# A fused RWKV, Mamba and feed-forward block on one core: in its first phase the reciprocal by Ln and Exp with a Newton step, the sigmoid by itself, the layer norm scaled by ScalarE, and the table lookups split seven to four

## The chip, the cores and the metric

The kernel runs on one core of one Trainium2 chip. A core has five engines with instruction queues of their own, each working in order: TensorE (PE, with its weight loads shown as PEld), VectorE (DVE), ScalarE (ACT), GpSimd (POOL) and SyncE (SP), which here issues the DMAs. An instruction that waits holds up all that is queued behind it on its engine. The metric is the device time of one execution in microseconds. Before the change the median of 3 runs is 3853.84 us (3852.79 to 3855.59).

## The reference

The input `x` has 4096 tokens (2 sequences of 2048) of 512 channels. Four residual parts follow each other, each behind a layer norm: an RWKV attention, a feed-forward, a Mamba, and the same feed-forward again. What the change touches is in the first part and in the weights of the second:

```python
def step(carry, kv):                       # RWKV, along the tokens
    p, q, o = carry
    kt, vt = kv
    no = jnp.maximum(o, u + kt)
    A = jnp.exp(o - no)
    Bc = jnp.exp(u + kt - no)
    y = (A * p + Bc * vt) / (A * q + Bc)
    no2 = jnp.maximum(w + o, kt)
    A2 = jnp.exp(w + o - no2)
    B2 = jnp.exp(kt - no2)
    return ((A2 * p + B2 * vt, A2 * q + B2, no2), y)
...
rvk = jnp.einsum('btc,dc->btd', x, W_rvk)
r, v, k = jnp.split(rvk, 3, axis=-1)
y = jax.nn.sigmoid(r) * wkv(time_decay, time_first, k, v)
return jnp.einsum('btc,dc->btd', y, W_out)
...
def _ghost_linear(x, idx, lut):            # feed-forward: weights from a table of 16 numbers
    w = lut[idx]
    return jnp.einsum('bsh,oh->bso', x, w)
...
h = jax.nn.silu(gate) * up
```

All tensors are float32. The denominator `A * q + Bc` is positive.

## The kernel before

The program has two phases. The second (Mamba and both feed-forwards, 16 chunks of 256 tokens, an order written out by hand with due times) is not touched. The first phase does the RWKV part in 8 chunks of 512 tokens (`TA`), and a scheduler orders its instructions on each engine, from the order of the code and its own estimates of durations.

A chunk begins with `layernorm_T`: DVE takes the statistics of four tiles of 128 tokens (L89, L90), POOL forms the reciprocal root `rs` (L91, L92), DVE scales the rows to `xn` (L95), PE transposes them (L98), ACT copies them to `xnT` (L99). Then a loop over `c` takes four groups of 128 channels; one pass of it is called a block here, and blocks are counted through from 0 to 31. In a block:

- PE projects k, r and v into PSUM (L293, 24 matmul passes);
- ACT takes `er` = exp(-r) (L303);
- DVE scans the running maximum `o` (L316) and forms `e`, the difference that all exponents come from (L320);
- ACT makes four Relu and Exp pairs from `e`: `b2`, `a2`, `bb`, `aaS` (L323 to L330), and copies `aaS` to `aa` in PSUM (L331);
- DVE multiplies with v (L333 `bv`, L334 `vb`) and scans p and q (L335, L336); ACT carries the last column on (L337, L312);
- POOL forms the numerator in `vb` (L339, L340);
- DVE forms the denominator in `aa` (L341, L342), multiplies it by 1 + `er` (L343), so that one reciprocal (L344) serves the division and the sigmoid together, and writes `yT` (L345).

At the end of a chunk PE multiplies `yT` with `wout` (L351), DVE adds to `x` (L353), and SP stores the chunk.

Beside that, the phase prepares the feed-forward's weights for the second phase: 11 pieces (`NF`) of 128 x 1536 indices are looked up in the table of 16 numbers and stored to DRAM as `wff`. There are two ways. `lookup` does it by bits on DVE: four masks from the index bits (L158), one product of masks (L161), and a nest of and/xor with polynomial coefficients (L167 to L184), 23 operations on 128 x 1536 integers. `lookup_pe` does it by products: DVE compares the indices with each of the values 0 to 15 (L211, one step each), and PE adds up nine matmuls for each step (L214) with diagonal matrices that hold three bfloat16 pieces of the table's numbers. Both are generators; `put`, called at the end of each block, takes so many steps of each as `lots` says. In the last four blocks `feed_forward` puts the first 256 tokens through the feed-forward (L248, L254, L238).

PSUM holds five buffers `mm` (k, r, v, `a2`, `aa` of a block in turn; also the transposes and the output products) and three `lk`. The tile pool `wk` holds eleven buffers for the other intermediates; `opq` (o, p, q) has two.

Of the kernel before, what the change touches and what calls it, by code (L numbers as in the profile page):

```python
# [8 lines left out]
F32 = mybir.dt.float32  # L9
I32 = mybir.dt.int32  # L10
AF = mybir.ActivationFunctionType
ALU = mybir.AluOpType
# [3 lines left out]
P = 128  # L16
# [5 lines left out]
NF = (FF + P - 1) // P  # L22
# [38 lines left out]
def block_kernel(ctx: ExitStack, tc: tile.TileContext, a: dict, out: bass.AP):  # L61
    nc = tc.nc
    V, S, G, PE = nc.vector, nc.scalar, nc.gpsimd, nc.tensor
# [18 lines left out]
    def layernorm_T(xt, n, xnT, small, new_xn, trp):  # L82


        st = small.tile([P, n, 6], F32, tag="st", name="st")
        mv = small.tile([P, n, 2], F32, tag="mv", name="mv")
        rs = small.tile([P, n, 1], F32, tag="rs", name="rs")
        for j in range(n):
            V.bn_stats(st[:, j, :], xt(j))  # L89
            V.bn_aggr(mv[:, j, :], st[:, j, :])  # L90
        G.tensor_scalar(rs, mv[:, :, 1:2], EPS, None, ALU.add)  # L91
        G.tensor_tensor(rs[:, :, 0], rs[:, :, 0], mhalf[:, :n], ALU.pow)  # L92
        for j in range(n):
            xn = new_xn()
            V.tensor_scalar(xn, xt(j), mv[:, j, 0:1], rs[:, j, :], ALU.subtract, ALU.mult)  # L95
            tr = trp.tile([P, KC, P], F32, tag="mm", name="tr")
            for k in range(KC):
                PE.transpose(tr[:, k, :], xn[:, k * P : (k + 1) * P], ident)  # L98
            S.copy(xnT[:, :, j * P : (j + 1) * P], tr)  # L99


    with ExitStack() as pa:
# [3 lines left out]
        small = pa.enter_context(tc.tile_pool(name="a_small", bufs=2))  # L106
# [20 lines left out]
        def load_x(i):  # L127
            xt = xp.tile([P, TA // P, C], F32, tag="x", name="x")
            nc.sync.dma_start(
                xt, a["x"][i * TA : (i + 1) * TA, :].rearrange("(j p) c -> p j c", p=P)  # L130
            )
            return xt
# [89 lines left out]
        def feed_forward():  # L222
# [4 lines left out]
            nc.sync.dma_start(xt, x1)  # L227
            xnT = lp.tile([P, KC, TB], F32, tag="fT", name="fT")
            layernorm_T(lambda j: xt[:, j, :], nj, xnT, small,
                        lambda: xnp.tile([P, C], F32, tag="xn", name="xn"), mmp)  # L230
            yield
# [32 lines left out]
        def each(how, part):  # L264
            for i in part:
                yield from how(i)

        lots = [(each(lookup, range(0, NF, 2)), 30, 0, 27), (each(lookup_pe, range(1, NF, 2)), 80, 0, 28),
                (feed_forward(), NF + 1, 28, 31)]

        def put(block):
            for steps, n, lo, hi in lots:
                if lo <= block < hi:
                    for _ in range(n * (block - lo) // (hi - lo), n * (block + 1 - lo) // (hi - lo)):
                        next(steps, None)
                if block == hi - 1:
                    for _ in steps:
                        pass
# [3 lines left out]
        for ci in range(nchunk):  # L282
            xt = first if ci == 0 else load_x(ci)
            xnT = xp.tile([P, KC, TA], F32, tag="xnT", name="xnT")
            layernorm_T(lambda j: xt[:, j, :], TA // P, xnT, small,
                        lambda: xnp.tile([P, C], F32, tag="xn", name="xn"), mmp)
            yT = xp.tile([P, KC, TA], F32, tag="yT", name="yT", bufs=1)
            for c in range(KC):
                def proj(which):
                    ps = mmp.tile([P, TA], F32, tag="mm", name="ps")  # L290
                    lo = which * C + c * P
                    for k in range(KC):
                        PE.matmul(ps, lhsT=wrvk[:, k, lo : lo + P], rhs=xnT[:, k, :],  # L293
                                  start=(k == 0), stop=(k == KC - 1))
                    return ps

                def t(name):
                    return wk.tile([P, TA], F32, tag="wk", name=name)

                k_ps, r_ps, v_ps = proj(2), proj(0), proj(1)  # L300
                w1 = wcol[:, c : c + 1]
                er = t("er")
                S.activation(er, r_ps, AF.Exp, scale=-1.0)  # L303

                st3 = wk.tile([P, 3, TA + 1], F32, tag="opq", name="opq", bufs=2)
                o, pp, qq = (st3[:, d, :] for d in range(3))
                if ci % (SEQ // TA) == 0:
                    V.memset(o[:, 0:1], -1e38)
                    V.memset(pp[:, 0:1], 0.0)
                    V.memset(qq[:, 0:1], 0.0)  # L310
                else:
                    S.copy(st3[:, :, 0], car[:, :, c])  # L312
                if c == 0:
                    nxt = carp.tile([P, 3, KC], F32, tag="car", name="car")
                old, new = slice(0, TA), slice(1, TA + 1)
                V.tensor_tensor_scan(o[:, new], w1.to_broadcast([P, TA]), k_ps, o[:, 0:1],  # L316
                                     ALU.add, ALU.max)

                e = t("e")
                V.scalar_tensor_tensor(e, o[:, old], w1, k_ps, ALU.add, ALU.subtract)  # L320
                a2, aa = (mmp.tile([P, TA], F32, tag="mm", name=n) for n in ("a2", "aa"))
                b2, bb, aaS = t("b2"), t("bb"), t("aaS")
                S.activation(b2, e, AF.Relu)  # L323
                S.activation(b2, b2, AF.Exp, scale=-1.0)
                S.activation(a2, e, AF.Relu, scale=-1.0)
                S.activation(a2, a2, AF.Exp, scale=-1.0)
                S.activation(bb, e, AF.Relu, bias=nwu[:, c : c + 1])
                S.activation(bb, bb, AF.Exp, scale=-1.0)
                S.activation(aaS, e, AF.Relu, bias=wu[:, c : c + 1], scale=-1.0)
                S.activation(aaS, aaS, AF.Exp, scale=-1.0)  # L330
                S.copy(aa, aaS)  # L331
                bv, vb = t("bv"), t("vb")
                V.tensor_tensor(bv, b2, v_ps, ALU.mult)  # L333
                V.tensor_tensor(vb, bb, v_ps, ALU.mult)  # L334
                V.tensor_tensor_scan(pp[:, new], a2, bv, pp[:, 0:1], ALU.mult, ALU.add)  # L335
                V.tensor_tensor_scan(qq[:, new], a2, b2, qq[:, 0:1], ALU.mult, ALU.add)  # L336
                S.copy(nxt[:, :, c], st3[:, :, TA])  # L337

                G.tensor_tensor(aaS, aaS, pp[:, old], ALU.mult)  # L339
                G.tensor_tensor(vb, aaS, vb, ALU.add)  # L340
                V.tensor_tensor(aa, aa, qq[:, old], ALU.mult)  # L341
                V.tensor_tensor(aa, aa, bb, ALU.add)  # L342
                V.scalar_tensor_tensor(aa, er, 1.0, aa, ALU.add, ALU.mult)  # L343
                V.reciprocal(aa, aa)  # L344
                V.tensor_tensor(yT[:, c, :], vb, aa, ALU.mult)  # L345
                put(KC * ci + c)
            car = nxt
            for j in range(TA // P):
                po = mmp.tile([P, C], F32, tag="mm", name="po")
                for k in range(KC):  # L350
                    PE.matmul(po, lhsT=yT[:, k, j * P : (j + 1) * P], rhs=wout[:, k, :],  # L351
                              start=(k == 0), stop=(k == KC - 1))
                V.tensor_tensor(xt[:, j, :], xt[:, j, :], po, ALU.add)  # L353
            nc.sync.dma_start(x1d[ci].rearrange("(j p) c -> p j c", p=P), xt)


    with ExitStack() as pb:
# [13 lines left out]
        small = pb.enter_context(tc.tile_pool(name="b_small", bufs=2))  # L371
# [437 lines left out]
        for w in range(-1, nchunk + 1):  # L809
            t = SLOTS * w  # L810
# [85 lines left out]
```

## Time and profile before

| | |
|---|---|
| median of 3 runs | 3853.84 us (3852.79 to 3855.59) |
| profiled execution | 3854.41 us |
| its span | 3852.6 us, 44708 instructions |
| busy in the span: PE, DVE, POOL, ACT | 93%, 84%, 71%, 67% |
| first phase, 0 to 805 us: PE, DVE, ACT, POOL busy | 706.7, 674.6, 256.2, 106.6 us |

A line of the page's chain of waits gives the lines on the way that ended last; a group line gives a source line, engine, operation, output and input tile with their shapes, the count, then busy time and mean nanoseconds of one, then the idle time of the engine just ahead of it and what ended that. Busy time counts overlapping instructions once, so that a group's busy time can be below its count times its mean. The 40 digits of an engine are its busy share in tenths in 40 equal slices of the span.

### The profile page before, as it was taken

To read this page: it belongs to the slowest core of one execution; us is meant where nothing else is said; L and a number is where in the kernel's file an instruction comes from. 1 tells how busy PE (TensorE), PEld (TensorE's weight loads), DVE (VectorE), ACT (ScalarE), POOL (GpSimd) and SP (SyncE) were. 2 spreads that over 40 slices of the span, in tenths; PEclk is the share of its full clock that TensorE was granted. 3 is DMA by queue.
4 is the path that set the end of the run, shared out by engine and by line. 5 is a ranking of instruction groups with operands and counts; after the bars stand their busy time and mean duration, and the time that the engine had idled before them with its cause. 6 is when DMAs were issued, how large, how long until landed. Compare 5 with 4: busy or idle time off the path is not lost.

```text
span 3852.6 us, 44708 instructions
## 1 busy us (share of the span) xinstructions
PE 3568.7 (93%) x13360; PEld 2425.7 (63%) x13360; DVE 3229.6 (84%) x5004; ACT 2593.7 (67%) x4631; POOL 2724.1 (71%) x2655
## 2 busy tenths in 40 slices
PE   7988799967899999999999999999999999999598
PEld 3433344535676777777767676767767767776375
DVE  8999997437888888888889898898888888888882
ACT  4323232337877878787878787878778787878661
POOL 1111111008889899989898999989898989899850
PEclk9999899988999999999999999999999999999799
DMA  2111110225456565656555555656565656563442
GB/s 107 60 38 63 55 47 30 77 93 182 152 172 198 171 196 168 194 171 197 167 184 187 184 178 181 191 176 193 171 198 171 194 170 194 170 196 114 148 147 61
DMA packets 266881, 572.58 MB, mean 149 GB/s; under 512 B 29840, under 2 KB 31504, under 8 KB 266640
## 3 DMA queue, kind: packets, MB, share of 16 engines
q1 hardware_dynamic: 266640, 569.73, 45.9%
q8 instruction: 107, 1.75, 0.2%
q14 instruction: 134, 1.10, 0.1%
HBM read 543.14 MB, written 26.48 MB: 148 GB/s over the span
## 4 chain that ended last, share of the span: by engine, by line
PE 38%; ACT 23%; POOL 18%; DVE 16%; issue 3%; DMA 1%; SPq 0%; POOLq 0%; DVEq 0%; ACTq 0%
PE po L503 13%; POOL db L716 8%; ACT h L726 6%; PE pg L523 5%; PE gu L523 5%; POOL db L746 4%; PE ps L706 4%; ACT L726 3%; POOL acc L751 3%; DVE aa L344 2%; PE ps L523 2%; PE ps L293 2%; PE y L769 1%; ACT ps L590 1%; DVE h L736 1%
## 5 line engine op out<-in xcount | busy, mean ns | idle before, releaser
L736 DVE TENSOR_TENSOR_SCAN h<-h,db 128x512 f32<-128x512 f32 x1024 | 1252.1, 1223 | 190.2 <-ACT h L726 129.1
L716 POOL TENSOR_TENSOR db<-du,bc 128x1024 f32<-128x1024 f32 x512 | 1206.1, 2356 | 41.8 <-PE y L759 41.8
L726 ACT ACTIVATE h<-dl,acol 128x256 f32<-128x256 f32 x2048 | 958.0, 475 | 344.9 <-DVE hst L739 307.9
L737 DVE TENSOR_TENSOR db<-h,bc 128x512 f32<-128x512 f32 x1024 | 708.0, 691 | 36.5 <-DVE h L736 0.5
L746 POOL TENSOR_TENSOR db<-db 128x512 f32<-128x512 f32 x480 | 609.5, 1270 | 20.2 <-DVE db L737 11.7
L503 PE MATMUL po<-w,hT 128*128 128x512 f32 x1364 | 600.6, 592 | 0.0
L523 PE MATMUL pg<-xnT,w 128*128 128x256 f32 x2480 | 553.5, 381 | 1.7 <-ACT xnT L483 1.4
L523 PE MATMUL gu<-xnT,w 128*128 128x256 f32 x2480 | 553.4, 379 | 0.0
L523 PEld LDWEIGHTS pg<-xnT,w 128*128 128x128 f32 x2480 | 472.0, 191 | 70.1 <-ACT xnT L483 6.7
L523 PEld LDWEIGHTS gu<-xnT,w 128*128 128x128 f32 x2480 | 472.2, 190 | 63.1
L339 POOL TENSOR_TENSOR aaS<-aaS,opq 128x512 f32<-128x512 f32 x32 | 34.9, 1091 | 602.6 <-DVE opq L335 547.0
L503 PEld LDWEIGHTS po<-w,hT 128*128 128x128 f32 x1364 | 259.6, 190 | 286.6 <-issue 273.5
L751 POOL TENSOR_TENSOR acc<-db 128x256 f32<-128x256 f32 x480 | 348.6, 726 | 37.6
L293 PE MATMUL ps<-xnT,wrvk 128*128 128x512 f32 x768 | 346.9, 606 | 14.8 <-ACT xnT L99 12.2
L726 ACT ACT_TABLE_LOAD x263 | 337.4, 1283 | 5.0 <-issue 0.4
L293 PEld LDWEIGHTS ps<-xnT,wrvk 128*128 128x128 f32 x768 | 149.2, 195 | 192.1 <-issue 167.0
L596 DVE SCALAR_TENSOR_TENSOR ps<-xin,cw,ps 128x256 f32<-128x256 f32 x384 | 185.7, 488 | 79.1 <-ACT ps L590 70.0
L576 PE MATMUL ps<-xnT,w 128*128 128x256 f32 x1024 | 246.2, 402 | 4.3 <-ACT xnT L483 4.3
L576 PEld LDWEIGHTS ps<-xnT,w 128*128 128x128 f32 x1024 | 207.6, 205 | 43.2 <-ACT xnT L483 6.5
L706 PE MATMUL ps<-xnT,w 128*128 128x256 f32 x1024 | 232.1, 383 | 1.4 <-ACT sg L712 1.4
L503 PE MATMUL po<-w,u 128*128 128x512 f32 x512 | 228.7, 595 | 0.0
L706 PEld LDWEIGHTS ps<-xnT,w 128*128 128x128 f32 x1024 | 197.3, 193 | 35.6 <-issue 6.5
(151 smaller groups left out, 4893.2 us busy)
## 6 DMA issues: line engine op xcount, KB each, us to landing
w<-wff SPq DMA_DIRECT2D x1023, 256.0 KB, 2.7
bc<-bcd SPq DMA_DIRECT2D x256, 512.0 KB, 4.3
w<-in_in_proj SPq DMA_DIRECT2D x256, 256.0 KB, 2.7
w<-in_out_proj SPq DMA_DIRECT2D x128, 256.0 KB, 2.8
wff<-t SPq DMA_DIRECT2D x11, 768.0 KB, 3.2
w<-wff SPq DMA_DIRECT2D x11, 768.0 KB, 4.2
x<-in_x SPq DMA_DIRECT2D x8, 1024.0 KB, 5.8
x1d<-x SPq DMA_DIRECT2D x8, 1024.0 KB, 4.5
```

Of the source, the lines that this page charges most:

```text
L293: PE.matmul(ps, lhsT=wrvk[:, k, lo : lo + P], rhs=xnT[:, k, :], start=(k == 0), stop=(k == KC - 1))
L503: PE.matmul(po[j], lhsT=lw[:, j * P : (j + 1) * P], rhs=w[i]["w"][:m], start=(i == 0), stop=(i == n - 1))
L523: PE.matmul(to[:m], lhsT=w[:, k, :m], rhs=box["xnT"][:, k, :], start=(k == 0), stop=(k == KC - 1))
L576: PE.matmul(ps[cp][:, j, :], lhsT=wj[:, k, :], rhs=box["xnT"][:, k, :], start=(k == 0), stop=(k == KC - 1))
L596: V.scalar_tensor_tensor(ps[cp][:, j, :], xin[cp][:, j, i : i + TB], cw[:, c, i : i + 1], ps[cp][:, j, :], ALU.mult, ALU.add)
L706: PE.matmul(ps[:, j, :], lhsT=wj[:, k, :], rhs=box["xnT"][:, k, :], start=(k == 0), stop=(k == KC - 1))
L716: G.tensor_tensor(d, box["du", half][:, c4, :].unsqueeze(1).to_broadcast([P, 4, TB]), bs[half, q], ALU.mult)
L726: S.activation(h[:, n, :], box["dl", half][:, c4, :], AF.Exp, scale=acol[:, 4 * half + c4, col : col + 1])
L736: V.tensor_tensor_scan(flat(h), flat(h), flat(d[:, two, :]), 0.0, ALU.mult, ALU.add)
L737: V.tensor_tensor(d[:, two, :], h, cs[half, q][:, two, :], ALU.mult)
L746: G.tensor_tensor(d[:, 0:2, :], d[:, 0:2, :], d[:, 2:4, :], ALU.add)
L751: G.tensor_tensor(acc[k], d[:, 0, :], d[:, 1, :], ALU.add)
```

## The change

Five edits, all in the first phase; the second phase's code is the same.

1. Layer norm: two small POOL operations form `nm` = -mean x rs, and ACT instead of DVE scales the rows, as rs x x + nm.
2. `er` is replaced by `sig` = sigmoid(r), from ACT's Sigmoid.
3. POOL multiplies the numerator by `sig`, a third product.
4. The reciprocal goes: ACT takes Ln of the denominator and Exp of minus that, as a first guess `rec`; DVE makes one Newton step with two three-operand products, which gives minus the denominator times the guess, then plus 2 and times the guess.
5. `lots`: the pieces 0, 2, 4, 5, 7, 8 and 10 are looked up by bits (35 steps over 27 blocks), the pieces 1, 3, 6 and 9 by products (64 steps over 28 blocks). Before it was the six even ones by bits and the five odd ones by products.

```diff
--- before.py
+++ after.py
@@ -90,9 +90,12 @@
             V.bn_aggr(mv[:, j, :], st[:, j, :])
         G.tensor_scalar(rs, mv[:, :, 1:2], EPS, None, ALU.add)
         G.tensor_tensor(rs[:, :, 0], rs[:, :, 0], mhalf[:, :n], ALU.pow)
+        nm = small.tile([P, n, 1], F32, tag="nm", name="nm")
+        G.tensor_tensor(nm, rs, mv[:, :, 0:1], ALU.mult)
+        G.tensor_scalar(nm, nm, -1.0, None, ALU.mult)
         for j in range(n):
             xn = new_xn()
-            V.tensor_scalar(xn, xt(j), mv[:, j, 0:1], rs[:, j, :], ALU.subtract, ALU.mult)
+            S.activation(xn, xt(j), AF.Identity, bias=nm[:, j, :], scale=rs[:, j, :])
             tr = trp.tile([P, KC, P], F32, tag="mm", name="tr")
             for k in range(KC):
                 PE.transpose(tr[:, k, :], xn[:, k * P : (k + 1) * P], ident)
@@ -265,7 +268,7 @@
             for i in part:
                 yield from how(i)
 
-        lots = [(each(lookup, range(0, NF, 2)), 30, 0, 27), (each(lookup_pe, range(1, NF, 2)), 80, 0, 28),
+        lots = [(each(lookup, (0, 2, 4, 5, 7, 8, 10)), 35, 0, 27), (each(lookup_pe, (1, 3, 6, 9)), 64, 0, 28),
                 (feed_forward(), NF + 1, 28, 31)]
 
         def put(block):
@@ -299,8 +302,8 @@
 
                 k_ps, r_ps, v_ps = proj(2), proj(0), proj(1)
                 w1 = wcol[:, c : c + 1]
-                er = t("er")
-                S.activation(er, r_ps, AF.Exp, scale=-1.0)
+                sig = t("sig")
+                S.activation(sig, r_ps, AF.Sigmoid)
 
                 st3 = wk.tile([P, 3, TA + 1], F32, tag="opq", name="opq", bufs=2)
                 o, pp, qq = (st3[:, d, :] for d in range(3))
@@ -336,12 +339,18 @@
                 V.tensor_tensor_scan(qq[:, new], a2, b2, qq[:, 0:1], ALU.mult, ALU.add)
                 S.copy(nxt[:, :, c], st3[:, :, TA])
 
+
+
                 G.tensor_tensor(aaS, aaS, pp[:, old], ALU.mult)
                 G.tensor_tensor(vb, aaS, vb, ALU.add)
+                G.tensor_tensor(vb, vb, sig, ALU.mult)
                 V.tensor_tensor(aa, aa, qq[:, old], ALU.mult)
                 V.tensor_tensor(aa, aa, bb, ALU.add)
-                V.scalar_tensor_tensor(aa, er, 1.0, aa, ALU.add, ALU.mult)
-                V.reciprocal(aa, aa)
+                rec = t("rec")
+                S.activation(rec, aa, AF.Ln)
+                S.activation(rec, rec, AF.Exp, scale=-1.0)
+                V.scalar_tensor_tensor(aa, aa, -1.0, rec, ALU.mult, ALU.mult)
+                V.scalar_tensor_tensor(aa, aa, 2.0, rec, ALU.add, ALU.mult)
                 V.tensor_tensor(yT[:, c, :], vb, aa, ALU.mult)
                 put(KC * ci + c)
             car = nxt
```

## The prediction

> **What bounds the kernel now.** I read the busy shares over the span first, then the first phase stage by stage, then the groups of that phase, then the order of single instructions in it. The page shows in 40 slices of 96.3 us where each engine works:
>
> ```profile
> PE   7988799967899999999999999999999999999598
> DVE  8999997437888888888889898898888888888882
> ACT  4323232337877878787878787878778787878661
> ```
>
> The first eight slices and a bit (to 805 us) are the phase that the change touches; behind it all four compute engines stand in the same order as before, row by row, so its roughly 3,045 us are taken over unchanged. Cut at the first `bv` (L333) of block 20 (521.6 us) and of block 28 (692.2 us; a block is one of 32 passes of the loop over `c`), the phase has three stages with different limits (columns: window; length; busy us and count of PE, PEld, DVE, ACT, POOL; clock; DMA share; GB/s):
>
> ```profile
> core 0: us, PE busy (x) PEld busy (x) DVE busy (x) ACT busy (x) POOL busy (x), PEclk, DMA share, GB/s
> 26.00:521.60 495.60, 436.79 (x1281) 193.14 (x1282) 481.91 (x511) 144.71 (x276) 69.09 (x50) 0.94 0.14 50
> 521.60:692.20 170.60, 159.99 (x476) 71.48 (x474) 127.20 (x151) 55.64 (x111) 25.86 (x22) 0.97 0.10 37
> 692.20:805.00 112.80, 106.19 (x331) 62.10 (x329) 52.98 (x59) 37.95 (x63) 9.63 (x9) 0.98 0.19 68
> ```
>
> Stage 1: DVE is busy 97%, so it is the bound, and a microsecond taken off it counts. Stages 2 and 3: PE is busy 94%, DVE 75% and 47%; there PE and the order of waits decide. The groups of the phase that the change concerns (busy us, mean ns, idle before):
>
> ```profile
> L344 DVE RECIPROCAL aa<-aa 128x512 f32<-128x512 f32 x32 | 107.3, 3353 | 0.3
> L343 DVE SCALAR_TENSOR_TENSOR aa<-er,aa 128x512 f32<-128x512 f32 x32 | 21.8, 682 | 0.2
> L95 DVE TENSOR_SCALAR xn<-x,mv,rs 128x512 f32<-128x512 f32 x32 | 16.7, 553 | 10.3 <-POOL rs L92 9.2 <-PE tr L98 1.1
> L211 DVE TENSOR_SCALAR one<-ixb 128x1536 bf16<-128x1536 bf16 x80 | 50.6, 645 | 1.5 <-ACT ixb L207 1.5
> L340 POOL TENSOR_TENSOR vb<-aaS,vb 128x512 f32<-128x512 f32 x32 | 56.6, 1768 | 2.5
> L303 ACT ACT_TABLE_LOAD x3 | 3.8, 1283 | 4.0 <-PE ps L293 4.0
> ```
>
> The reciprocal is DVE's largest group. ACT seldom changes its table: 11 loads in the phase, almost all for the feed-forward's Silu. And one block of stage 2, with a table load of stage 3 (start, length, engine):
>
> ```profile
> 631.04 0.69 DVE L343 SCALAR_TENSOR_TENSOR aa<-er,aa 128x512 f32<-128x512 f32 x1
> 632.11 3.36 DVE L344 RECIPROCAL aa<-aa 128x512 f32<-128x512 f32 x1
> 636.48 0.66 DVE L345 TENSOR_TENSOR yT<-vb,aa 128x512 f32<-128x512 f32 x1
> 639.53 0.69 DVE L333 TENSOR_TENSOR bv<-b,ps 128x512 f32<-128x512 f32 x1 [1.73 <-ACT b L324]
> ...
> 628.12 10.46 PE L293 MATMUL ps<-xnT,wrvk 128*128 128x512 f32 x24
> 638.42 5.99 PE L214 MATMUL lk<-one,pieces 128*128 128x512 bf16 x27
> ...
> 750.16 1.28 ACT L330 ACT_TABLE_LOAD   x1
> 751.45 0.63 ACT L330 ACTIVATE aaS<-aaS 128x512 f32<-128x512 f32 x1
> ```
>
> A block of stage 2 takes 16.1 us, and PE fills it: 10.4 us of projections and 5.7 us of lookup products.
>
> **What the skill says.** "ScalarE: Activation LUTs", What ACT_TABLE_LOAD costs, gives 1283 ns for a load and some 1380 ns of drain with every switch. The trace agrees on 1283 ns, but the activation follows 0.01 us after the load: I take 1.28 and keep 2.66 for a rival. The same page, section Table sets, says that one set holds both exp and ln; the built order of the changed kernel nevertheless loads ahead of `Ln` and again ahead of `Exp`, so that saving is not had; no run here shows it. "SBUF — State Buffer", SBUF: two separate sides, says that GpSimd and certain DVE operations exclude each other for a whole instruction. The trace agrees: the `one` at 629.38 us took 1.02 us under a POOL product (527 ns at its fastest), and L340 runs from 1.26 to 2.70 us.
>
> **The change, part by part.** All places are from the built order of the changed kernel; all durations from this trace.
>
> DVE's sum in stage 1, to `bv` of block 20. Both orders have 551 instructions there, so means may be subtracted.
> - 20 reciprocals go: -67.1. A second three-operand product comes for each: 20 x 0.682 = +13.6.
> - 24 `xn` go to ACT: 24 x 0.553 = -13.3.
> - 11 fewer `one` (50 instead of 61): -7.1.
> - Lookups by bits, 23 operations and 35.4 us each by their means: seven whole ones instead of six less their last five operations (8.5 us): +43.7. Four more row statistics stand before the mark, +2.7.
> The sum is -27. Little, because the relieved engine gets a seventh lookup.
>
> Waits of DVE that go: `xn` on POOL's `rs`, 6.5 us in stage 1, some 2 of them at the start, where ACT now does `xn` between its `pieces` and the first projection starts later; I count -4, and +1 for that start. POOL gets a third product, 1.46 us like L340's median, 20 times in stage 1. Its own time is free (69 us busy in 496), but it holds DVE up. In before DVE's stretched operations (L211 by 0.1 on 80, L181 by 0.24, others less) add some 12 us for 92 us of POOL products; 29 us more make +4.
>
> A new wait: `Ln` starts when `aa` has its second sum, and the first Newton product waits for `Exp`. On ACT that is 0.66 (Ln with its wait) + 1.29 (load) + 0.61 (Exp) + 0.1 (semaphores, overlap) = 2.67 us. DVE is in order: behind the waiting product stand `e` of the next block, `yT`, lookup pieces and `bv`, and for `e` waits ACT, for `yT` PE. Between the second sum and that product the order has one lookup piece, a scan, or `one`s: by the means 1.4 to 3.2 us, 2.2 on average. Summing the shortfalls block by block gives 14 us. In four blocks more lies on ACT's way (three where the load of the Ln table itself carries the wait, one where the sigmoid and its load stand before `Exp`): +4. Later in the block `bv` and `vb` find their exponentials ready in all but two blocks: +1. Together +19. The bounds: nothing, if lookups slide in better than I read, and +19 more at twice the shortfall.
>
> Stage 1 in all: -27 - 4 + 1 + 4 + 19 = -7.
>
> Stage 2. PE loses 0.7 `one` step a block (1.95 us each): 10.4 + 4.4 = 14.8 us. But the ring of waits is now longer. From `bv` at 0: scan 0.8, `vb` 2.3 (waits for exp of `bb`), scan 2.9, `one` 4.05, `aa` to 5.3. ACT's copy of the carry (L312) waits for that `aa`; only then comes the Ln load, to 6.85; Ln, load, Exp to 9.4; products 9.45 and 10.2, `yT` 10.9, `e` 11.5 to 12.2; two Relus, a load, Exp: 15.3 us to the next `bv`. The sigmoid and its load (done at 11.3) lie beside the products. Six intervals inside the chunks took 99.3 us (16.3, 18.2, 17.0, 16.2, 15.6, 16.0), and 6 x 15.3 = 91.8: -7. The two chunk borders (34.7 and 36.7) stay with PE; four `xn` between copies on ACT cost each some 0.5: +1. Stage 2: -6.
>
> Stage 3. The 62 us of feed-forward matmuls (38.0 + 3.7 of `gu`, 18.5 + 2.0 of `po`) set the pace beside the projections; Silu, with one or two more loads around it, is ready before PE's next `gu` in every step I followed (closest: 0.7 us). At the end `yT` of block 31 comes 0.5 us later, and PE has 8 products ready instead of 10 for the wait (0.86 us each): +2.
>
> At nothing: ACT's added work (124 more loads at 1.28, 64 activations at 0.6, 34 `xn` at 0.81 as in L477: 225 us), which its idle time takes (256 us busy in 805) apart from the round trip above; the sigmoid in place of `er`, which waits for `r_ps` as `er` did (152 us idle there); the two small POOL steps for `nm`, which stand most of a block ahead of `xn` and would cost some 1.3 us a chunk uncovered (0.24 and 1.04 us, as L91 and L92). SP issues the same eleven index loads and eleven stores; a store waits for its lookup and holds up what is queued behind it, the next `x` load among it, as before, when `x` was late by 1.1 us once in stage 1.
>
> Sum: -7 - 6 + 2 = -11 against the profiled execution's 3854.41 (span 3852.6 and 1.8 around it), 0.6 above the median 3853.84. I say 3842.
>
> **Rivals.**
> - Full relief: the round trip is hidden, stage 1 gives -30, stage 2 falls to PE's 14.8 (-10), stage 3 stays: 3814. For it: DVE has lookup pieces everywhere in stage 1. Against: the order has mostly one in the gap.
> - Slower: the round trip DVE-ACT-DVE is longer than 2.67 us. It stands bare in about 30 of 32 blocks, so each microsecond more costs 30. From 0.4 us on it eats the gain, from 0.65 it shows as slower. With the drain of 1.38 it is 3842 + 41 = 3883; half of it, 3863. For it: stage 2 has no filler at all. Against: no such drain shows around a load.
> - Nothing to measure: PE's 94% in stages 2 and 3 leaves only stage 1's -7: 3847.
>
> **How the numbers follow.** A measurement of this kernel tells about 0.2%, 7.7 us: faster is below 3846.1, slower above 3861.5. Likeliest case with its bounds, 3826 to 3859, 0.45; full relief 0.22; slower 0.20; nothing 0.13. Below 3846.1 lie 0.30 of the likeliest, all of full relief and 0.04 of the last: 0.56. Above 3861.5 lie four fifths of the slower case and a few hundredths of the rest: 0.20. Same: 0.24. The range for 8 in 10 reaches to both rivals: 3813 to 3872.
>
> **What would show it.** Right: about 135 table loads in the first phase; the first Newton product idle on ACT `rec` for 0.3 to 1.3 us in most blocks, some 18 us before block 20, 1.5 to 2.7 in each block of stage 2; `bv` of block 20 near 514, block intervals of 15 us after it, stage 3 of equal length. Wrong: no such idle time (full relief), gaps beside the loads or DVE idle of 3 us and more a block (slower), or PE waiting in stage 3 for Silu.

## The result, and the profile after

The changed kernel takes 3862.53 us (3860.09 to 3864.99) where the kernel before takes 3854.75 in the same series: a ratio of 1.0022, with a 95% interval of 1.0013 to 1.0031. It is 7.8 us slower; 11 us faster was forecast. Its profiled execution took 3860.09 us with a span of 3858.3, 5.7 above that of before. From the last addition to `x` in the first phase to the end of the span both take 3048.2 us, so all of the difference lies in the first phase.

The 40 slices of the span after the change:

```profile
PE   6888889967899999999999999999999999999598
DVE  7999975327898888888889888898888888888882
ACT  6655566437878878777878787878778787878661
```

Against the digits before the change, DVE's first and its sixth to ninth fell, ACT's first eight rose, and of PE's first seven three fell and one rose: the work went from DVE to ACT, and PE got no denser. The stages and the whole phase (columns: window; length; busy us and count of PE, PEld, DVE, ACT, POOL; clock; DMA share; GB/s), after and then before:

```profile
26.00:516.00 490.00, 410.76 (x1177) 181.83 (x1176) 458.95 (x515) 287.28 (x417) 115.64 (x84) 0.94 0.14 53
516.00:688.05 172.05, 154.96 (x443) 69.15 (x442) 91.61 (x123) 112.19 (x167) 33.38 (x33) 0.94 0.08 28
688.05:810.10 122.05, 110.97 (x331) 64.52 (x329) 42.27 (x58) 58.24 (x84) 14.52 (x12) 0.94 0.18 63
0.00:810.10 810.10, 679.42 (x1956) 317.84 (x1956) 603.35 (x731) 477.05 (x719) 166.04 (x139) 0.94 0.16 58
```

```profile
0.00:804.40 804.40, 706.70 (x2100) 329.71 (x2100) 674.03 (x759) 256.16 (x501) 106.39 (x89) 0.96 0.16 59
```

PE has 27.3 us less to do, as one lookup by products went, and is idle for 130.7 us instead of 97.7. DVE has 70.7 us less to do. Neither shortened the phase. By its marks:

| us | before | after | difference | forecast |
|---|---|---|---|---|
| first `bv` | 39.6 | 44.3 | +4.7 | +1 (within the next row) |
| stage 1, to `bv` of block 20 | 521.6 | 516.0 | -5.6 | -7 |
| stage 2: six intervals inside chunks | 99.2 | 94.3 | -4.9 | -7 |
| stage 2: two chunk borders | 71.3 | 77.7 | +6.4 | +1 |
| stage 3, to the last addition to `x` | 112.2 | 122.0 | +9.8 | +2 |
| sum | 804.4 | 810.1 | +5.7 | -11 |

The groups that answer to those of before (busy us, mean ns of one, idle time before and what ended it):

```profile
L346 POOL TENSOR_TENSOR vb<-vb,sig 128x512 f32<-128x512 f32 x32 | 49.3, 1541 | 2.5
L306 ACT ACT_TABLE_LOAD x32 | 41.1, 1283 | 4.5 <-PE ps L296 4.0
L350 ACT ACT_TABLE_LOAD x32 | 41.1, 1283 | 15.8 <-DVE aa L348 15.4
L351 ACT ACT_TABLE_LOAD x32 | 41.1, 1283 | 0.6
L327 ACT ACT_TABLE_LOAD x31 | 39.8, 1283 | 0.5
L98 ACT ACTIVATE xn<-x,nm,rs 128x512 f32<-128x512 f32 x32 | 25.1, 816 | 18.6 <-POOL nm L95 18.6
L352 DVE SCALAR_TENSOR_TENSOR aa<-aa,rec 128x512 f32<-128x512 f32 x32 | 22.4, 699 | 55.9 <-ACT rec L351 55.8
```

Four tables are loaded in every block but one, which has three, and the first Newton product (L352) waits 55.8 us in all for `rec`: 20.2 in stage 1, 21.3 in stage 2, 14.3 in stage 3.

A chunk border of stage 2, from the timeline (start, length, engine; in brackets the idle time before; the xN at the end counts what is called records below, single matmul passes), before and after:

```profile
572.78 5.99 PE L214 MATMUL lk<-one,pieces 128*128 128x512 bf16 x27
578.61 5.31 PE L351 MATMUL po<-wout,yT 128*128 128x512 f32 x12
585.14 8.85 PE L351 MATMUL po<-wout,yT 128*128 128x512 f32 x20 [1.22 <-DVE yT L345]
```

```profile
563.73 2.74 PE L360 MATMUL po<-wout,yT 128*128 128x512 f32 x6
567.12 1.99 PE L360 MATMUL po<-wout,yT 128*128 128x512 f32 x4 [0.66 <-DVE vb L337]
575.54 9.47 PE L360 MATMUL po<-wout,yT 128*128 128x512 f32 x16 [6.43 <-DVE yT L354]
...
569.40 1.28 ACT L350 ACT_TABLE_LOAD   x1
570.69 0.60 ACT L350 ACTIVATE rec<-aa 128x512 f32<-128x512 f32 x1
571.31 1.28 ACT L351 ACT_TABLE_LOAD   x1
572.60 0.63 ACT L351 ACTIVATE rec<-rec 128x512 f32<-128x512 f32 x1
...
569.10 0.70 DVE L348 TENSOR_TENSOR aa<-aa,bb 128x512 f32<-128x512 f32 x1
573.26 0.70 DVE L352 SCALAR_TENSOR_TENSOR aa<-aa,rec 128x512 f32<-128x512 f32 x1 [3.46 <-ACT rec L351]
```

Three things are to be seen. The wait for `rec` is bare, that is, DVE has nothing else to do in it: 3.46 us. From `bv` on (573.05 us before, 564.12 after) PE has ten records to do ahead of `yT` where it had 39, as the scheduler laid 20 lookup records ahead of `bv`, and it stands idle for 6.43 us instead of 1.22. `yT` itself starts 10.7 us after `bv`, where before it was 11.4, so a later `yT` is not the reason here. (At the other border it is 10.7 instead of 9.9.) And then 16 records take 9.47 us, 0.59 each, where 20 took 8.85 before, 0.44 each: after the idle time PE runs at a lower clock. The other border is alike (7.29 us idle, then 18 records in 10.77).

Stage 3 shows it once more, after the change and in one of the experiments below, which keeps `er`:

```profile
691.05 1.13 PE L296 MATMUL ps<-xnT,wrvk 128*128 128x512 f32 x2 [2.31 <-DVE vb L337]
693.84 10.08 PE L251 MATMUL gu<-fT,w 128*128 128x256 f32 x32 [1.66 <-ACT fT L102]
...
691.35 0.58 ACT L102 COPY fT<-tr 128x512 f32<-128x512 f32 x1
692.23 0.20 ACT L340 COPY car<-opq 128x3 f32<-128x3 f32 x1 [0.29 <-DVE opq L339]
693.11 0.20 ACT L315 COPY opq<-car 128x3 f32<-128x3 f32 x1 [0.68 <-DVE aa L347]
693.21 0.58 ACT L102 COPY fT<-tr 128x512 f32<-128x512 f32 x1
```

```profile
700.59 1.12 PE L296 MATMUL ps<-xnT,wrvk 128*128 128x512 f32 x2 [1.94 <-DVE vb L337]
701.55 7.07 PE L251 MATMUL gu<-fT,w 128*128 128x256 f32 x32
```

In the changed kernel the second copy to `fT` stands behind two copies of the carry in ACT's queue, of which the second waits for DVE. So `gu` waits 1.66 us more, and the same 32 matmuls take 10.08 us instead of 7.07. The granted clock in that place, in windows of PE alone (window; length; busy; clock):

```profile
688.00:692.00 4.00, 1.69 (x9) 1.00 0.00 0
694.00:698.00 4.00, 4.00 (x10) 0.50 0.00 0
698.00:702.00 4.00, 4.00 (x16) 0.78 0.00 0
702.00:706.00 4.00, 4.00 (x15) 1.00 0.01 2
```

The interval from block 28 to 29 grew by 5.1 us: 2.0 of waiting and 3.0 of half clock. At the end of the phase PE is idle for 3.74 us ahead of the last 16 records, where before all 32 output records ran through without a stop in 14.21 us, and these 16 take 8.83 us where 7.03 is the full rate.

### The profile page after: what moved, and what is told of

It is laid out like the page before. It is cut to its first block, busy times and chain, and to the rows that moved or that the text cites. A ratio compares the mean times of both kernels' runs of the same rounds, so it can differ in the third digit from the quotient of the medians.

```text
span 3858.3 us, 44667 instructions
## 1 busy us (share of the span) xinstructions
PE 3538.4 (92%) x13216; PEld 2407.3 (62%) x13216; DVE 3158.7 (82%) x4977; ACT 2819.0 (73%) x4849; POOL 2786.5 (72%) x2705
## 4 chain that ended last, share of the span: by engine, by line
POOL 40%; PE 22%; DVE 17%; ACT 15%; issue 5%; DMA 1%; SPq 0%; POOLq 0%; DVEq 0%; ACTq 0%
POOL db L725 17%; POOL db L755 9%; POOL acc L760 5%; PE po L512 4%; DVE h L745 4%; PE gu L532 4%; PE pg L532 3%; ACT h L735 3%; POOL db L759 3%; DVE db L746 2%; PE ps L296 2%; POOL db L728 1%; ACT L735 1%; POOL du L673 1%; PE ps L715 1%
## 5 line engine op out<-in xcount | busy, mean ns | idle before, releaser
L755 POOL TENSOR_TENSOR db<-db 128x512 f32<-128x512 f32 x480 | 610.1, 1271 | 20.1 <-DVE db L746 11.7
L735 ACT ACT_TABLE_LOAD x263 | 337.4, 1283 | 4.7
L585 PEld LDWEIGHTS ps<-xnT,w 128*128 128x128 f32 x1024 | 205.8, 203 | 44.3 <-ACT xnT L492 7.6
```

Source lines behind the costliest of these rows:

```text
L585: PE.matmul(ps[cp][:, j, :], lhsT=wj[:, k, :], rhs=box["xnT"][:, k, :], start=(k == 0), stop=(k == KC - 1))
L735: S.activation(h[:, n, :], box["dl", half][:, c4, :], AF.Exp, scale=acol[:, 4 * half + c4, col : col + 1])
L755: G.tensor_tensor(d[:, 0:2, :], d[:, 0:2, :], d[:, 2:4, :], ALU.add)
```

## The experiments

All are compared with the kernel before on the same chip; `us` is the difference of the medians. The kernels ran in several series, so two of them are compared by their differences from the kernel before. The marks are of each one's profile, that is, of one execution.

| kernel | us | ratio, 95% | first `bv` | `bv` of 20 | stage 2 | stage 3 |
|---|---|---|---|---|---|---|
| changed | +7.8 | 1.0022 (1.0013, 1.0031) | 44.3 | 516.0 | 172.1 | 122.0 |
| u_recip | +4.9 | 1.0016 (1.0009, 1.0022) | 44.8 | 520.9 | 165.1 | 122.4 |
| u_lots65 | +10.3 | 1.0029 (1.0017, 1.0040) | 44.8 | 511.4 | 181.6 | 122.7 |
| u_ln_dve | -2.8 | 0.9994 (0.9986, 1.0002) | 41.8 | 506.4 | 169.7 | 122.0 |
| u_keep_er | +5.5 | 1.0014 (1.0007, 1.0020) | 44.1 | 521.9 | 176.0 | 113.3 |
| v_last_old | -3.3 | 0.9992 (0.9985, 0.9998) | 44.7 | 517.4 | 171.7 | 111.6 |
| v_new_until_20 | -19.8 | 0.9946 (0.9934, 0.9959) | 41.6 | 504.2 | 167.6 | 111.8 |
| v_borders_old | -5.4 | 0.9986 (0.9980, 0.9993) | 40.8 | 514.9 | 170.2 | 112.9 |
| v_b_ln | -17.4 | 0.9953 (0.9940, 0.9965) | 43.0 | 500.2 | 171.8 | 111.2 |
| w_b_form | +14.7 | 1.0038 (1.0024, 1.0052) | 40.9 | 518.0 | 177.6 | 121.0 |
| w_b_lots | +26.1 | 1.0063 (1.0051, 1.0076) | 39.4 | 540.3 | 175.4 | 112.6 |
| w_all_but_form | +31.6 | 1.0081 (1.0068, 1.0095) | 42.8 | 549.3 | 173.7 | 111.2 |
| w_new_until_20_ln | -8.4 | 0.9977 (0.9968, 0.9986) | 45.5 | 513.7 | 167.2 | 111.3 |
| x_spread | -0.2 | 1.0000 (0.9992, 1.0008) | 45.0 | 504.3 | 175.1 | 122.6 |
| x_ln_late | +0.6 | 1.0001 (0.9993, 1.0009) | 41.4 | 508.5 | 172.5 | 123.1 |
| x_ln_early | +2.8 | 1.0008 (0.9999, 1.0016) | 45.7 | 516.0 | 165.7 | 121.7 |
| x_b_ln_spread | -35.8 | 0.9905 (0.9892, 0.9919) | 42.9 | 483.4 | 170.8 | 113.8 |
| y_new_until_20_spread | -28.4 | 0.9926 (0.9912, 0.9939) | 41.1 | 498.9 | 164.0 | 112.9 |
| y_new_until_20_ln_spread | -34.2 | 0.9909 (0.9895, 0.9922) | 44.4 | 503.9 | 153.2 | 112.6 |

**Each edit undone by itself.** The reciprocal again (u_recip):

```diff
-                rec = t("rec")
-                S.activation(rec, aa, AF.Ln)
...
+                V.reciprocal(aa, aa)
```

> The changed kernel with the reciprocal on DVE again in place of Ln, Exp and the two Newton products; all else as changed (72 table loads instead of 135). In both theories stage 1 (to bv of block 20) loses what the change saved there: 20 x (3.35 - 2 x 0.68) = +40 us of DVE less the 20 us that DVE waits for rec: about +20. Round-trip theory (PE stands idle at the chunk borders of stage 2 and at the end because yT comes late through ACT): PE's idle before po falls from 6.4 and 7.3 us to 2 or less, the two borders go from 38.3 and 39.5 to about 35, block 28 to the last x add from 122 to 114: in all +20 - 8 - 8 = +4 against the changed kernel. Fill theory (yT is only 1.4 us later by the round trip; PE idles because fewer lookup products and po products stand ahead of yT): the idle falls by 1.4 us only, borders 37 and 38, the last stage -2: in all +20 - 3 - 2 = +15.

Measured: 2.9 us less than the changed kernel, below both theories. Stage 2 falls by 6.9 as the round-trip theory has it, with borders of 33.2 and 36.5: at the first PE has 37 records ahead of `yT` again and no idle time to speak of, while the second keeps its 7.3 us, nearer to the other theory; stage 3 does not fall at all. Both theories were wrong for stage 1: it grew by 4.9 us, not 20. Some of the steps of the lookups by bits that the changed kernel does there moved to blocks 20 and 21 (DVE is busy for 117 us in stage 2, not 92: 10 more for these steps, 15 for the reciprocals). The mark at block 20 is no fixed frame: time taken off DVE ahead of it can be refilled with steps from behind it.

The lookups six to five again (u_lots65):

```diff
-        lots = [(each(lookup, (0, 2, 4, 5, 7, 8, 10)), 35, 0, 27), (each(lookup_pe, (1, 3, 6, 9)), 64, 0, 28),
+        lots = [(each(lookup, range(0, NF, 2)), 30, 0, 27), (each(lookup_pe, range(1, NF, 2)), 80, 0, 28),
```

> The changed kernel with the lookups split six by bits and five by products again. DVE has 35.4 - 10.3 = 25 us less to do, PE 31 us more. Fill theory: PE's idle before po at the two borders of stage 2 falls to 2 us or less, borders about 36; stage 1 shorter by 15 to 20 (DVE is its bound), stage 2 inner intervals back near 16.5 (+5); in all -8 to -15 against the changed kernel, so faster than before the change. Round-trip theory: with fewer lookup pieces to cover it the wait for rec grows in stage 1 from 20 to 35 us, borders stay at 38 and 39; in all -2 to +8.

Measured: +2.5 against the changed kernel. PE's idle time at the borders falls to 3.6 and 4.8 us, not to 2, and the borders do not shorten (39.4 and 41.1). The sum is in the range of the round-trip theory, but its reason is not seen: the wait for `rec` in stage 1 fell to 17.7. Missing products are not the whole of the idle time.

The layer norm on DVE again (u_ln_dve), and `er` kept (u_keep_er):

```diff
-            S.activation(xn, xt(j), AF.Identity, bias=nm[:, j, :], scale=rs[:, j, :])
+            V.tensor_scalar(xn, xt(j), mv[:, j, 0:1], rs[:, j, :], ALU.subtract, ALU.mult)
```

> The changed kernel with the layer norm's rows scaled on DVE again, without the two small POOL steps. Theory that ACT's layer norm is what costs (it stands in ACT's queue behind other copies at the start and at every border): first bv at 40 instead of 44.3, each border shorter by 1 to 2 us, block 28 to 29 back from 32.9 to 28; 32 xn add 17 us to DVE, 13 of them in stage 1: -4.5 + 9 - 3 - 5 = -4. Theory that it costs only at the start: first bv at 40, borders and block 28 to 29 as changed: -4.5 + 11 = +6.

```diff
-                S.activation(sig, r_ps, AF.Sigmoid)
+                S.activation(er, r_ps, AF.Exp, scale=-1.0)
...
-                G.tensor_tensor(vb, vb, sig, ALU.mult)
...
+                V.scalar_tensor_tensor(aa, er, 1.0, aa, ALU.add, ALU.mult)
```

> The changed kernel without the separate sigmoid: er = exp(-r) is kept, a three-operand product by (1 + er) goes ahead of Ln, POOL's third product goes (78 table loads instead of 135, since no load is needed between er and the other exponentials). Theory that the loads as such cost: DVE's wait of bv for b (27 us in all) goes, and with it about 10 us of the time, mostly in stages 2 and 3: -10. Round-trip theory: the path from the second sum to yT is 0.7 us longer in every block, the load ahead of b is 1.3 shorter: stage 1 +5 (14 us more on DVE, 4 back from POOL's product, some waits less), stage 2 inner -3, borders +1, end +0.7: +2 to +4.

Measured: the layer norm is the edit whose undoing gains most, 10.6 us, more than either theory had; 2.5 at the start, 7 between there and block 20, 2.3 in stage 2, nothing in stage 3. Keeping `er` brings stage 3 back to 113.3, with no late `fT` and no `gu` at half clock, but costs 6 us up to block 20 and 4 in stage 2. The sum, 2.3 us below the changed kernel, lies between the theories: `bv` waits for `b` for 6 us instead of 27, but that is worth far less than 10.

**Where the new form costs.** "New form" is the sigmoid apart, Ln, Exp, Newton and POOL's third product. In blocks 28 to 31 the form of before (v_last_old):

```diff
+                old_form = ci == nchunk - 1
+                if old_form:
+                    S.activation(sig, r_ps, AF.Exp, scale=-1.0)
...
+                if old_form:
+                    V.scalar_tensor_tensor(aa, sig, 1.0, aa, ALU.add, ALU.mult)
+                    V.reciprocal(aa, aa)
```

> The changed kernel, but in blocks 28 to 31 the form of before: er = exp(-r), product by (1 + er), reciprocal on DVE, no third product on POOL. Theory that the two forms differ in stage 3 by what PE loses there (the sigmoid's extra load delays ACT so that gu waits for fT, the late yT of block 31, and half the clock after each idle stretch): from bv of block 28 to the last x add 112 to 113 us instead of 122.0, no gu of 10 us in the place of 7, so -9 against the changed kernel. Theory that stage 3 is long because of ACT's layer norm: the 32 gu still wait for fT and take 10 us, stage 3 stays above 118, so -3 or less.

Measured: 11 us less than the changed kernel, stage 3 at 111.6 and no `gu` of 10 us: the first theory, in its place, and a little more in size.

The same edit with another condition, from block 20 on, with the layer norm on DVE (v_new_until_20) or on ACT (w_new_until_20_ln), or in the last block of each chunk and in blocks 28 to 31 (v_borders_old):

```diff
+                old_form = ci >= nchunk - 3
```

> The new form (sigmoid, Ln, Exp, Newton, POOL's third product) in blocks 0 to 19 alone, where DVE is the bound; the form of before in blocks 20 to 31; layer norm on DVE; lookups seven to four as changed. Theory that the new form helps only where lookup pieces cover its wait and DVE is the bound: bv of block 20 at 506 (as with the layer norm on DVE), stage 2 163 us (PE's 152.6 and some 10 idle) instead of 169.7, stage 3 112: last x add at 781 to 784, 20 to 23 us before that of the kernel before: 3831 to 3834. Theory that the wait is not the point and PE idles in stage 2 for want of lookup products: stage 2 stays at 169 or more, last x add at 788 or later: 3838 or more.

> The new form in blocks 0 to 19, the form of before in blocks 20 to 31, lookups seven to four, and the layer norm on ACT (on DVE this gave 3833.6, 19.8 less than before). Theory that the form and ACT's layer norm do not go together in stage 1: bv of block 20 at 516 to 517 as with the change (504 with the layer norm on DVE), stage 2 163 to 167, stage 3 112: last x add 792 to 795, -9 to -12 against before. Theory that the layer norm's gain adds as it did on the kernel before: last x add 766 to 772, -33 to -38 against before.

```diff
+                old_form = ci == nchunk - 1 or c == KC - 1
```

> As the last one, but the form of before in the last block of every chunk and in blocks 28 to 31; the new form elsewhere, in blocks 20 to 22 and 24 to 26 too; layer norm on DVE. Theory that only the borders and stage 3 lose by the new form: borders of stage 2 35 and 35 or less, PE's idle before po there 4 us or less, inner intervals as with the layer norm on DVE (97.6 in all): stage 2 166, stage 3 112, stage 1 508 to 512 (five reciprocals more): 3836 to 3842. Theory that PE's idle at the borders comes from missing lookup products: idle before po stays at 5.5 us (the reciprocal way is only 1.4 us shorter), borders 72 in all, stage 2 170: 3842 to 3848.

Measured: the last addition to `x` comes at 783.6 in v_new_until_20 and at 792.2 in w_new_until_20_ln, in each a figure of the first theory, though stage 2 of v_new_until_20 is 167.6 us, between the two; against the kernels with the new form in all blocks that is 17 and 16 us. In v_borders_old the idle time at the borders stays at 3.9 and 6.9 us and the borders at 74.7 in all, so the second theory is the nearer one: the reciprocal in the border block alone does not give PE its work back, and the five reciprocals in stage 1 cost more than expected.

**Each part by itself on the kernel before.** The layer norm on ACT (v_b_ln), the new form (w_b_form), the lookups seven to four (w_b_lots), and all but the form (w_all_but_form); the edits are those of the change.

> The kernel before with one edit of the change alone: the layer norm's rows scaled on ACT, with the two small POOL steps. Theory that ACT's layer norm costs by itself, being late at the start and at the borders: first bv 3 to 5 us later, borders 1 to 2 longer each, and the 13 us saved on DVE in stage 1 do not outweigh it: 0 to +8 against before. Theory that it costs only together with the loads that crowd ACT: stage 1 shorter by 13 + 5 of waits for rs less 4 at the start, borders as before: -10 to -14 against before.

> The kernel before with the new form alone (sigmoid apart, Ln, Exp, Newton, POOL's third product) in all blocks; layer norm on DVE, lookups six to five as before. With the layer norm on ACT the form cost 28 us on top (3863.8 against 3836.0). Theory that the form costs by itself (it makes the way through a block longer, and DVE's saved time is spent waiting): +20 to +28 against before. Theory that form and ACT's layer norm are in each other's way in ACT's queue: without it stage 1 gains what DVE is relieved of, 53 us less 30 of waits, stages 2 and 3 lose 10 each: -5 to +3 against before.

> The kernel before with the lookups split seven to four, nothing else. DVE +25 us, PE -31 us. Theory that DVE is the bound up to block 20 and what does not fit moves to blocks 20 to 23, where DVE has room: stage 1 +12 to +20, stage 2 -5 to -10, stage 3 0: +5 to +12 against before. Theory that PE's saved products are had in full: -10 or less.

> Layer norm on ACT and lookups seven to four, with the form of before (er, reciprocal) in all blocks: the change without its first and second edit. Theory that each part acts for itself: layer norm -17, lookups +5 to +12: -5 to -12 against before. Theory that the layer norm's relief of DVE pays for the seventh lookup, so that both gains are had: -20 or less. Theory that ACT's layer norm is good only while DVE is overloaded: with the seventh lookup DVE is more so, -15 to -20.

With the three above, this gives every combination of form, layer norm and lookups, in us against before:

| | lookups 6 to 5 | lookups 7 to 4 |
|---|---|---|
| form of before, layer norm on DVE | 0 | +26.1 |
| form of before, layer norm on ACT | -17.4 | +31.6 |
| new form, layer norm on DVE | +14.7 | -2.8 |
| new form, layer norm on ACT | +10.3 | +7.8 |

Nothing adds. Form and lookups each cost alone and cancel together; the layer norm on ACT gains 17 on the kernel before and costs 10.6 on top of the other two. In v_b_ln the theory of a cost of its own fell; w_b_form came between its theories, and in the last two every theory was below what came. In w_b_lots DVE, with a seventh lookup and all reciprocals, is busy for 490 of the 501 us from the first `bv` to that of block 20, and so carries that mark to 540. In w_all_but_form it has 15 us less to do there, stands idle for 32 us, and the mark still comes at 549; why is not shown.

**Where the lookup pieces lie.** A piece is here one step of a lookup, not one of the 11 pieces of the weights. A lookup by bits yields four times, so six of them have 24 steps, and seven 28; but they are dealt out in 30 and 35 shares over 27 blocks. So they run out at four fifths of the way, by the code in block 21; in the order of the changed kernel the last of them starts in block 19. x_spread changes that one number in the changed kernel, x_b_ln_spread in v_b_ln (24 for 30):

```diff
-        lots = [(each(lookup, (0, 2, 4, 5, 7, 8, 10)), 35, 0, 27),
+        lots = [(each(lookup, (0, 2, 4, 5, 7, 8, 10)), 28, 0, 27),
```

> The changed kernel with one number changed: the 28 steps of the seven lookups by bits are dealt out over blocks 0 to 26 in 28 shares instead of 35, so that they last longer (up to block 21 instead of 19 in the order). Theory that ACT's layer norm costs because the time it frees on DVE only pulls lookup pieces forward, so that none is left to cover the wait for rec after block 19: DVE's wait for rec in stage 2 falls from 21 to 17 us or less, -7 to -10 against the changed kernel. Theory that it costs in ACT's queue, whatever DVE does: -3 to +3.

> A candidate: the kernel before with the layer norm on ACT (3836.0) and its 24 lookup steps by bits dealt out in 24 shares instead of 30, so that pieces last up to block 25. Theory that what counts is that DVE's lookup work lies where DVE has room: stage 1 shorter by 15 to 20, stage 2 longer by 5: 3821 to 3828. Theory that the order of pieces is of no account while their sum is the same: 3834 to 3838.

Measured: x_spread is 8.0 us below the changed kernel, as the first theory said, but not in its way: the wait for `rec` in stage 2 is 22.5 us, not 17. The gain is in stage 1, 11.7 us, where PE's idle time from the first `bv` on fell from 78.0 to 49.6. The one number moved more than the steps by bits: 58 of the 64 comparisons `one` now come before block 20, not 50, and stage 2 grew by 3.1. x_b_ln_spread gains more than either theory had, 18.4 us over v_b_ln; stage 1 is 16.8 shorter, and stage 2 no longer at all. The two windows of each, v_b_ln and then x_b_ln_spread:

```profile
42.99:500.16 457.17, 413.55 (x1245) 183.31 (x1244) 455.97 (x478) 153.81 (x288) 75.26 (x60) 0.96 0.15 52
500.16:671.96 171.80, 160.50 (x477) 71.79 (x475) 121.59 (x140) 62.66 (x121) 24.85 (x28) 0.97 0.10 37
```

```profile
42.94:483.38 440.44, 410.04 (x1226) 183.90 (x1248) 433.85 (x461) 153.44 (x289) 70.05 (x60) 0.97 0.15 52
483.38:654.22 170.84, 158.43 (x460) 70.41 (x466) 148.66 (x159) 62.55 (x120) 29.05 (x28) 0.96 0.11 42
```

In v_b_ln DVE is busy for 456 of 457 us up to block 20 and for 122 of 172 after it. The new number moves 27 us of pieces over that line (121.6 to 148.7), PE's busy time in stage 2 stays, and the phase is shorter by 15 us in the profile. The profile's other 4 us lie behind the phase and are not explained.

The layer norm on ACT in chunks 5 to 7 and the feed-forward alone (x_ln_late), or in chunks 0 to 4 alone (x_ln_early), in the changed kernel:

```diff
+            if on_act:
                 S.activation(xn, xt(j), AF.Identity, bias=nm[:, j, :], scale=rs[:, j, :])
+            else:
+                V.tensor_scalar(xn, xt(j), mv[:, j, 0:1], rs[:, j, :], ALU.subtract, ALU.mult)
```

> The changed kernel with the layer norm on DVE in chunks 0 to 4 (stage 1), on ACT in chunks 5 to 7 and the feed-forward. First theory (lookup pieces pulled forward, and the start): as with the layer norm on DVE throughout, -9 to -12 against the changed kernel, first bv at 41.8. Second theory (late in ACT's queue at the borders after block 19): -3 to -6, borders of stage 2 as changed (38.3 and 39.5).

> The counterpart: the layer norm on ACT in chunks 0 to 4, on DVE in chunks 5 to 7 and the feed-forward. First theory: the cost is made before block 20, so it stays: 0 to -3 against the changed kernel, first bv at 44 to 45, bv of block 20 at 515 to 518. Second theory: borders of stage 2 fall to 36 each or less: -4 to -8.

Measured: 7.2 and 5.0 us below the changed kernel, between the theories for x_ln_late and the second one's for x_ln_early, whose borders are 37.3 and 34.9. So it costs in both stages; 2.8 of it at the start, where ACT's `pieces` stand ahead of `xn`.

The new form until block 20, with the steps in 28 shares and either layer norm:

> The new form in blocks 0 to 19, the form of before after them, lookups seven to four, layer norm on DVE (3833.6 without the next edit), and the steps by bits dealt out in 28 shares instead of 35, so that pieces last up to block 24. Theory that the place of the pieces is worth the same here as on the kernel before: stage 1 -12 to -20, stage 2 +5: 3816 to 3824, close to the 3814.7 of the candidate without the new form. Theory that the new form needs the pieces in stage 1 as cover for its wait: DVE's wait for rec in stage 1 rises from 16 to 25 us or more, 3828 or more.

> The same with the layer norm on ACT (3843.0 without the spread). Theory that the layer norm's cost within the change is a matter of where the pieces lie: spread, it costs nothing more, 3816 to 3826. Theory that it costs in ACT's queue and at the start: 7 to 10 us more than the kernel of the same call with the layer norm on DVE.

Measured: 3824.4 us, 8.6 gained over v_new_until_20, at the edge of the first theory but not in its way: stage 1 gave 5.3, not 12 to 20, and stage 2 fell by 3.6. Against the second theory, the wait for `rec` in stage 1 fell from 16.3 to 13.1. With the layer norm on ACT it is 3818.6: now ACT's layer norm gains 5.8 us where it cost 11.4 without the spread. Its price is thus not fixed but turns on how the pieces are dealt out. What in the order makes it so, block by block, was not taken apart and stays open.

x_b_ln_spread, with the layer norm on ACT and 24 shares, gains as much (35.8 us against 34.2, with intervals that overlap), and it has neither the new form nor the seventh lookup. So the runs show no need of the form once the pieces are well laid. Whether the form until block 20 would gain on top of x_b_ln_spread was not measured.

## Why the prediction was wrong

- *Stage 1, -7: held (-5.6), and so did most of its parts.* DVE's busy time from 26 us to `bv` of block 20 fell by 23.0, and -27 with +4 for POOL's third product was the forecast. The wait for `rec` was 20.2 where 14 + 4 was forecast. The start was mis-sized: +4.7 instead of +1, as on ACT the second and third `xn` stand behind two batches of `pieces` of 4.8 us each, and the fourth behind those two, `ixb` and two copies.
- *Stage 2, inner intervals, -7: -4.9.* The last two took 15.2, the earlier ones 15.8 to 16.6; 15.3 had been forecast for each. The wait for `rec` in stage 2, 2.7 us a block, was at the upper end of the 1.5 to 2.7 named.
- *Stage 2, "The two chunk borders (34.7 and 36.7) stay with PE", +1: this step failed (+6.4).* PE stood idle for 6.4 and 7.3 us. The forecast took PE's time at the border as filled and priced ACT's `xn` alone. It looked neither at how many records PE has left ahead of `yT` (10 instead of 39 at the first border) nor at what idle time does to the clock. The reciprocal by itself put back brings both borders to their old length; put back in the border blocks alone, with the layer norm on DVE, it does not. So which edits take PE's work away there, and by what order, is in part open.
- *Stage 3, "Silu ... is ready before PE's next `gu` in every step I followed", "+2": this step failed too (+9.8).* PE's one wait ahead of a `gu` for what follows Silu is 2.41 us, the same as before; what was late was the second copy to `fT`, behind a carry copy that waits for DVE, and it was the sigmoid's form that put it there: keeping `er` takes it away, the reciprocal does not. At the end `yT` comes 12.0 us after `bv` instead of 10.9, and PE has 16 records (8 products, as forecast) ready and 16 to do at a lower clock. v_last_old shows that the form in these four blocks costs all of it.
- *A term was missing in both: the half clock.* The Trainium skill states it: "TensorE: Matmul & The Clock Gate", Part 1: The HAM clock gate, has PE's clock halved after a window of about 3.4 us without work, and full again after as much time at work, in windows that run on by themselves. The trace agrees on the half, with 0.50 granted from 694 to 698 us; but it does not take a window without work, since in the 3.41 us ahead of the change PE was still busy for 1.13. Counted against the full rate it is 2.4 and 2.8 us at the two borders, 3.0 at `gu` and 1.8 at the end: 10 of the 16 us by which the borders and stage 3 grew. (The second border has 1.7 more at its projections, and before the change had 1.6 of its own.)
- *The rival "slower" named a longer round trip.* That is part of it: bare, the wait is 3.46 us where 2.67 was the forecast with the load for Ln out of the way, since that load starts only 0.4 us before the second sum ends. Over the 32 blocks it is 3.45 us or more in six (one of stage 1, the two at the borders, three of stage 3) and 2.3 to 3.0 in eight more, not bare in 30; and no trace here shows the drain that this rival was priced with.
- *The premise that a microsecond off DVE counts in stage 1* gave the right sum for this change and would have misled on each part: the parts were added up, and they do not add. Nor was DVE's work in stage 1 a fixed sum: 27 us of it could be laid behind block 20, as x_b_ln_spread shows.

## What to carry to other kernels

Where an engine is full in one stage and has room in the next, look first at what deals the movable work out: one number of shares was worth 18 us alone and decided whether another edit gained or cost. Price a later hand-over to PE as the idle time plus, as here, up to two slots of half clock behind it (3.41 us each, worth 1.7 us of work; see the last section), and count what PE still has in hand when it starts to wait. Run the parts of a composite change in combination before adding up their prices.

## What the hardware showed that was not expected

An idle time of PE need not reach 3.4 us to cost the clock, and its length alone does not decide. Ahead of `gu`, 2.31 and 1.66 us with 1.13 us of matmuls between them were enough. Before the change 2.19 us alone made the 24 records behind it take 12.26 us, 0.51 each. In x_spread 3.35 us alone cost nothing: 19 records in 8.42 us, 0.44 each.

What decides can be read from the profiles. In all 20 the granted clock changes only at the borders of a grid of slots of 3.41 us, and each slot's clock follows what PE did in the slot before. PE alone in such slots (window; length; busy; clock), before the change and in x_spread:

```profile
663.37:666.78 3.41, 1.22 (x4) 1.00 0.46 189
666.78:670.19 3.41, 3.41 (x6) 0.50 0.00 0
```

```profile
598.84:602.25 3.41, 1.82 (x5) 1.00 0.00 0
602.25:605.67 3.42, 1.66 (x4) 1.00 0.00 0
605.67:609.08 3.41, 3.41 (x9) 1.00 0.00 0
```

The 2.19 us fell into one slot and left PE busy for 36% of it; the 3.35 us fell across two and left 53% and 49%. Between 40 and 800 us of the 20 profiles, by their count of PE's busy time, all 229 slots at full clock with PE busy for less than 35% were followed by half clock, and none of the 3546 with 60% or more; of the 168 between, 45 were. At half clock, all 251 slots with 85% or more were followed by full clock, and none of the 212 with less than 70%.

The slots lie differently in each profile, so the same idle time can cost one at half clock, 1.7 us of PE's work, in one profile and nothing in another: behind the same idle time of 1.16 us after transposes, 21 projection records took 10.98 us in v_b_ln and 9.28 in u_recip. So a difference of that size between the marks of two profiles need not come from an edit.

The compiled kernel loads a table ahead of Ln and again ahead of Exp, 32 times each (L350, L351), though "ScalarE: Activation LUTs", Table sets, names one set that holds both. Each load took 1283 ns, and in 111 of the phase's 135 loads the next activation followed within 0.01 us.
